# Sixteen images on two lanes: instructions numbered by their place in an image's course, images set 820 units apart, instead of by program order

## The chip, the cores and the metric

The kernel runs on one core of a Trainium2 chip. The metric is the device time of one execution in microseconds (us), lower is better. Engines are named as in the profile: PE (matrix multiplies), DVE (vector), ACT (activations), POOL (GpSimd) and SP (which here only issues DMAs).

## The reference, cut to what matters

The input is sixteen images of 56 x 56 tokens with 128 channels, float32. Each image goes through four residual layers, and nothing is shared between images:

```python
x = x + window_attention(_gn(x))   # 64 windows of 7x7, shifted, 4 heads
x = x + triangle(_gn(x))           # layer norm, gated product over one axis, layer norm, gate
x = x + fourier(_gn(x))            # spectral Q, K, V; 32-head attention; inverse transform; 2 spectral MLP layers
x = x + bilinear(_gn(x))           # SiLU MLP, 3x7 convolutions, per-token 16x16 products
```

`_gn` is a group norm over 32 groups of 4 channels. All arithmetic is float32.

## The kernel before, in words

`tile_blocks` writes out all sixteen images, one after the other, as straight-line code of 5065 numbered instructions each: load, window attention (from number 58), triangle (from 980), Fourier (from 1797), bilinear with the store (from 3668). These numbers are counted within an image, in the order in which the Python code issues them.

Image b uses **lane** `b % 2`. A lane has its own working storage: one arena of 17152 floats per partition (pool `arena`, one buffer), five small row tiles (`w2`), eight statistics tiles, and half of the PSUM banks (`psb`, two buffers, and `psd`, one). So two images can be under way at a time, one on each lane, and image b+2 can begin its arena work only when image b gives up the arena at its end. The lanes share the engines and the DMA queues. Each lane alone is a chain: within an image a stage needs the result of the one before, and inside a stage small buffers hold loops to two or three steps ahead.

Where the pieces of a stage stand, by line of the kernel before:

- window attention: eight window rows (loop over `wi`), L536 (normalise, on DVE and POOL), L538 to L607 (products and transposes on PE). It moves no data but the image.
- triangle: L628 to L722, products L678 and L698, no DMA.
- Fourier: the statistics and column modes (L907), `attention` with the products L1093, the spectral loop of eight steps, where POOL issues two table loads for each of 64 tiles (L1201), DVE multiplies them (L1203) and PE reduces them (L368 and L371, the helper `together`), then inverse transforms and two MLP layers (`operator`, L989, L945).
- bilinear: `project` (L1315 to L1366), `kept` (a tile is copied by ACT and written to DRAM eight times, L1316), `spread` (L1378), `contract` (SP loads the replicated tile, L1411, DVE multiplies, L1414, PE reduces through `together`).

**What sets the order.** The program is built with `schedule_with_timeline_sim=True`. At build time a list scheduler lays out each engine's queue: when an engine falls free in its model of time, of the instructions whose inputs and buffers are ready the one with the lowest number goes next. The number is `tc.cur_priority`, counted up by one with each instruction issued. In the kernel before nothing sets it, so it is program order: every instruction of image b has a lower number than every instruction of image b+1. The queues that come out are fixed; on the chip each engine runs its own in order and waits where a semaphore is not there yet.

Of the kernel before, what the change touches and what calls it, by code (L numbers as in the profile page):

```python
# [54 lines left out]
ROWC = NW * WIN  # L55
NEG = -1.0e30
SN = math.sqrt(28.0 * 64.0)


def _rho(r, cut):  # L60
# [247 lines left out]
def tile_blocks(ctx: ExitStack, tc: tile.TileContext, ins, out, at, stages=(0, 1, 2, 3)):  # L308
# [17 lines left out]
    ps2 = [pool(f"ps2_{k}", 1, space=PSUM) for k in range(2)]  # L326

    lane = [0]
    count = [0]

    def uid(s):
# [117 lines left out]
    def store_image(b, xt):  # L449
        for q in range(NCH):  # L450
# [8 lines left out]
                in_=t[:TT, :].rearrange("p (a c) -> p a c", a=4),  # L459
            )  # L460

    env = dict(locals())
    blocks = [_window_attention, _triangle, _fourier, _bilinear]
    run = {s: blocks[s](env) for s in stages}
    for b in range(NB):
        lane[0] = b % 2
        xt = load_image(b)
        done = False
        for s in stages:
            done = run[s](b, xt)  # L470
        if not done:
            store_image(b, xt)
# [7 lines left out]
def _window_attention(env):  # L480
    e = _Env(env)
# [34 lines left out]
    def run(b, xt):  # L516
# [8 lines left out]
        for k in range(2):  # L525
            nc.gpsimd.memset(ar[:, k * half_arena + ROWC : k * half_arena + 408], 0.0)
        for wi in range(NW):
            o = wi % 2 * half_arena
            xw, qt, vt, st, atn, ot = (
                ar[:, o + a : o + a + n]  # L530
# [84 lines left out]
def _triangle(env):  # L615
    e = _Env(env)
    nc, mm, tt, ts, act, C, W, bc = e.nc, e.mm, e.tt, e.ts, e.act, e.C, e.W, e.bc
    eps = e.persistent("eps1", [P, 1], 1e-5)
    HC = 32

    def layer_norm(chunk, dst, sqs, lw, lb):


        for q in range(NCH):
            d, sq = dst[:, q * CH : (q + 1) * CH], sqs[:, q * CH : (q + 1) * CH]
            src = chunk(q)
            p = e.psb()
            mm(p[:, :CH], lhsT=C("cen"), rhs=src, start=True, stop=True)  # L628
            act(sq, p[:, :CH], AF.Square)  # L629
            nc.vector.tensor_copy(d, p[:, :CH])  # L630

        pv = e.psb()
        e.together(
            dict(
                out=pv[32 * (q % 4) : 32 * (q % 4) + 32, :CH],
                lhsT=C("oh")[:, 1 - q // 4 : 33 - q // 4],
                rhs=sqs[:, q * CH : (q + 1) * CH],
                start=q < 4,
                stop=q > 2,
            )  # L640
            for q in range(NCH)
        )
        rs = e.w2()
        act(rs[:, :CH], pv[:, :CH], AF.Sqrt, bias=eps)
        nc.vector.reciprocal(rs[:, :CH], rs[:, :CH])
        for q in range(NCH):
            d = dst[:, q * CH : (q + 1) * CH]
            p = e.psb()
            row = 32 * (q % 4) + q // 4
            mm(p[:, :CH], lhsT=C("ident")[:, row : row + 1].to_broadcast([P, P]), rhs=rs[:, :CH], start=True, stop=True)  # L650
            tt(d, d, p[:, :CH], ALU.mult)
            act(d, d, AF.Identity, bias=W("ln")[:, lb : lb + 1], scale=W("ln")[:, lw : lw + 1])

    def run(b, xt):
        nm, rs = e.group_norm(xt)
        ar = e.arena()
        xh = ar[:, 0:3144]
        nc.gpsimd.memset(xh[:, NTOK:], 0.0)

        def normed(q):  # L660
            t = e.w2()
            ts(t[:, :CH], xt[:, q * CH : (q + 1) * CH], nm, rs, ALU.add, ALU.mult)
            return t[:, :CH]

        sqs = ar[:, 10312 : 10312 + NTOK]
        layer_norm(normed, xh, sqs, 0, 1)

        l3, r3 = (ar[:, o : o + T * HC].rearrange("p (c i) -> p i c", i=T) for o in (3144, 4936))  # L670
        o3 = ar[:, 6728 : 6728 + 64 * T].rearrange("p (j c) -> p c j", c=64)
        for part in range(2):
            for g in range(T // 8):
                p = e.psd()
                for i in range(8):
                    c0 = (8 * g + i) * T
                    for half, w in ((0, "w1a"), (64, "w1b")):
                        mm(  # L678
                            p[half : half + 64, i // 4, i % 4 * P : (i % 4 + 1) * P],
                            lhsT=xh[:, c0 : c0 + 64],  # L680
                            rhs=W(w).rearrange("p (k c) -> p k c", c=64)[:, :, HC * part : HC * part + HC],
                            start=True,
                            stop=True,
                        )
                pv = p.rearrange("p a (i c) -> p (a i) c", c=P)
                sg = e.w2()
                s3 = sg.rearrange("p (i c) -> p i c", c=64)
                act(s3, pv[:, :, 64:128], AF.Sigmoid)
                tt(l3[:, 8 * g : 8 * g + 8, :], pv[:, :, 0:32], s3[:, :, 0:32], ALU.mult)
                nc.vector.scalar_tensor_tensor(  # L690
                    r3[:, 8 * g : 8 * g + 8, :], pv[:, :, 32:64], 1.0 / T, s3[:, :, 32:64], ALU.mult, ALU.mult
                )
            for g in range(4):
                for half in (0, 64):
                    p = e.psb()
                    s = slice(half, half + T)
                    for c in range(8):
                        mm(p[s, c * T : (c + 1) * T], lhsT=l3[s, :, 8 * g + c], rhs=r3[s, :, 8 * g + c], start=True, stop=True)  # L698
                    dst = o3[s, 8 * (4 * part + g) : 8 * (4 * part + g + 1), :]
                    src = p[s, :CH].rearrange("p (c j) -> p c j", j=T)  # L700
                    if half:
                        nc.scalar.copy(dst, src)
                    else:
                        nc.vector.tensor_copy(dst, src)

        on = ar[:, 3144 : 3144 + NTOK]
        on3 = on.rearrange("p (i j) -> p j i", j=T)
        for g in range(T // 8):
            p = e.psb()
            for j in range(8):  # L710
                for half in (0, 64):
                    s = slice(half, half + T)
                    mm(p[half : half + 64, j * T : (j + 1) * T], lhsT=o3[s, :, 8 * g + j], rhs=C("ident")[s, half : half + T], start=True, stop=True)
            nc.scalar.copy(on3[:, 8 * g : 8 * g + 8, :], p[:, :CH].rearrange("p (j i) -> p j i", i=T))
        layer_norm(lambda q: on[:, q * CH : (q + 1) * CH], on, sqs, 2, 3)
        for q in range(NCH):
            s = slice(q * CH, (q + 1) * CH)
            pg, py = e.psb(), e.psb()
            mm(pg[:, :CH], lhsT=W("gout"), rhs=xh[:, s], start=True, stop=True)
            mm(py[:, :CH], lhsT=W("pout"), rhs=on[:, s], start=True, stop=True)  # L720
            sg = e.w2()
            act(sg[:, :CH], pg[:, :CH], AF.Sigmoid)  # L722
            tt(sg[:, :CH], py[:, :CH], sg[:, :CH], ALU.mult)
            tt(xt[:, s], xt[:, s], sg[:, :CH], ALU.add)

    return run


def _fourier(env):
    e = _Env(env)  # L730
# [145 lines left out]
    def inorm(y, k):  # L876

        _, rs = centered(y)
        ts(rs, rs, sc[:, k : k + 1], None, ALU.mult)
        scaled(y, y, rs, k)  # L880
# [144 lines left out]
    def attention(uv, ar):  # L1025
# [3 lines left out]
        for s in range(2):  # L1029
# [4 lines left out]
            t = e.w2()  # L1034
# [7 lines left out]
        t = e.w2()  # L1042
# [20 lines left out]
        for name in ("dx", "dya", "dyb"):  # L1063
# [6 lines left out]
            else:  # L1070
                t = e.w2()
# [9 lines left out]

        n = 0
        for bank in range(2):
            sp = e.psb()
            for l0 in (0, 4):
                for c in range(2):
# [41 lines left out]
        for g in range(2):  # L1128
            p = e.psb()
            for i in range(4):  # L1130
                q = 4 * g + i
# [7 lines left out]
            ts(by_row(dst)[:, s], by_row(xt)[:, s], nm, rs, ALU.add, ALU.mult)  # L1139

    def run(b, xt):
        nm, rs = e.group_norm(xt)
        ar = e.arena()
        xa = ar[:, 7056:10640]
# [8 lines left out]


        x3 = ar[:TT, : 3 * NM].rearrange("p (k n) -> p k n", k=3)
        for g in range(8):
            p = e.psb()
            for i in range(4):
# [28 lines left out]
        spec = x3[:, 0, :]  # L1187
        n = 0
        for q in range(8):
            s = slice(q * STEP, (q + 1) * STEP)  # L1190
            if q % 2:
                pa, pb = e.psb(), e.psb()
# [4 lines left out]
            for two in range(8):  # L1197
                t = slots[n % 8]
# [28 lines left out]
            nc.scalar.copy(spec[:, s], p)  # L1227


        y = ar[:, NM : NM + NTOK]  # L1230
        normed(xt, nm, rs, y)
        y3 = y.rearrange("p (t j) -> p j t", j=T)
# [12 lines left out]
        def residual(t0, p):  # L1245
            d = y[:, t0 * T : (t0 + 8) * T]
            tt(d, p, d, ALU.add)

        vs = ar[:, 5376 : 5376 + 4 * CH]
        inverse(ar, [spec], residual, vs)  # L1250
        an = ar[:, 5376:8960]
# [4 lines left out]
        p12 = ar[:, 8960:12544]  # L1256
        f = ar[:, 0:3584]
        vs = ar[:, 3584:5376]
        operator(ar, an, "mw0r", "mw0i", f, p12, f, vs, 3)
        nc.gpsimd.memset(by_row(f, True), 0.0)  # L1260
        for q in range(NCH):
            an8, f8 = (by_row(t)[:, 8 * q : 8 * q + 8] for t in (an, f))
            stt(f8, an8, sc[:, 12:13], f8, ALU.mult, ALU.add)
            act(f8, f8, AF.Gelu, bias=shift)
        m = an
        operator(ar, f, "mw1r", "mw1i", m, p12, m, vs, 4, sc[:, 14:15])
        for q in range(NCH):
            m8, f8 = (by_row(t)[:, 8 * q : 8 * q + 8] for t in (m, f))
            stt(m8, f8, sc[:, 14:15], m8, ALU.mult, ALU.add)
        inorm(m, 5)  # L1270
        for q in range(NCH):
            x8, m8 = (by_row(t)[:, 8 * q : 8 * q + 8] for t in (xt, m))
# [5 lines left out]
def _bilinear(env):  # L1278
    e = _Env(env)
# [9 lines left out]
    part = 96 * PLANE // P // 3  # L1289
# [7 lines left out]
        return bass.AP(tensor=t.tensor, offset=t.offset + start, ap=[list(d) for d in dims])  # L1297

    def run(b, xt):
        nm, rs = e.group_norm(xt)  # L1300
        ar = e.arena()
        kv_dram = padded[e.lane[0]]
# [151 lines left out]
        queries, kern, feat = {q: project(q) for q in range(2)}, {}, {}  # L1454
        spread(0, 0)
        for q in range(NCH + 4):
            if 0 <= q - 4:
                last(q - 4, *feat.pop(q - 4))
            if q + 2 < NCH:
# [39 lines left out]
```

## Time and profile before

| | |
|---|---|
| median of 5 runs | 13248.37 us |
| lowest, highest | 13231.01, 13284.84 us |
| profiled execution: time, span | 13248.37 us, 13246.3 us |
| mean granted TensorE clock | 0.859 |
| PE busy, share of the span | 10304.3 us, 78% |
| DVE busy | 9629.6 us, 73% |
| ACT, POOL busy | 3848.2 us (29%), 1619.6 us (12%) |
| DMA moved | 2105.99 MB, mean 159 GB/s |

The span is what the profile covers; the profiled execution took 2.1 us more than its span, and was the median run. Busy times of different engines overlap. A stretch "a:b" is in us from the start of the span. The first records of the even images (lane 0) start at 18, 1577, 3196, 4773, 6442, 8101, 9773 and 11354 us, those of the odd images (lane 1) at 22, 1647, 3285, 4966, 6670, 8359, 9954 and 11618 us; image 14 ends at 13036 us and image 15 at 13243 us. The images 2k and 2k+1 are called pair k+1, so there are pairs 1 to 8, and stretch k+1 runs from the start of image 2k to that of image 2k+2 (the eighth to the end).

### The profile page before, as it was taken

What the parts mean: (1) busy time and instruction counts of PE and PEld (TensorE: products, weight loads), DVE (VectorE), ACT (ScalarE), POOL (GpSimd) and SP (SyncE); (2) the same over time, 40 slices, a digit from 0 to 9 for tenths busy, and PEclk for the clock granted to TensorE, in tenths of its full rate; (3) what the DMA queues carried; (4) which work ended last, traced back from release to release, by engine and by line L of the source; (5) the groups of instructions that cost most, each with busy time, mean ns of one, the idle gap of its engine ahead of it and who ended that gap; (6) DMA issues with size and microseconds to landing.
All of it is one profiled execution on the core that took longest, in us unless ns stands there. A gap on an engine that the chain in (4) does not pass through costs nothing. (4 is left out here: it accounts for less than half of the span.)

```text
span 13246.3 us, 203312 instructions
## 1 busy us (share of the span) xinstructions
PE 10304.3 (78%) x82624; PEld 5717.4 (43%) x82624; DVE 9629.6 (73%) x13985; ACT 3848.2 (29%) x6643; POOL 1619.6 (12%) x3098
## 2 busy tenths in 40 slices
PE   7887688876877777877778777788777887778876
PEld 4443254532544335444354443444335443355432
DVE  7776868768677686676767767777686777767777
ACT  4223141321423214223242232422224222232221
POOL 0130002200022000220002200022000220002200
PEclk9888898888988888887888878998888888888888
DMA  1256904478044780446814458243680447804478
GB/s 35 66 174 228 320 4 118 122 256 295 1 125 120 248 292 11 122 114 222 292 38 124 116 192 292 68 124 116 227 306 19 125 123 240 280 27 121 127 239 290
DMA packets 1091764, 2105.99 MB, mean 159 GB/s; under 512 B 98320, under 2 KB 974096, under 8 KB 1089680
## 3 DMA queue, kind: packets, MB, share of 16 engines
q1 hardware_dynamic: 560000, 823.95, 18.9%
q0 software_dynamic: 165120, 629.61, 17.3%
q10 hardware_dynamic: 365712, 639.44, 13.3%
q8 instruction: 654, 10.72, 0.3%
q14 instruction: 278, 2.28, 0.1%
HBM read 1412.73 MB, written 667.03 MB: 157 GB/s over the span
## 5 line engine op out<-in xcount | busy, mean ns | idle before, releaser
L1414 DVE TENSOR_TENSOR arena<-arena 128x1792 f32<-128x1792 f32 x1344 | 2661.4, 2020 | 685.0 <-DMA arena<-dy 325.9
L1203 DVE TENSOR_TENSOR arena<-arena 112x1344 f32<-112x1344 f32 x1024 | 1570.0, 1553 | 338.2 <-DMA arena<-table 331.0
L371 PE MATMUL psb<-arena,cst 128*32 128x448 f32 x9792 | 1554.8, 662 | 0.8 <-ACT arena L629 0.8
L368 PE MATMUL psb<-arena,cst 128*32 128x448 f32 x1408 | 808.1, 662 | 801.4 <-DVE arena L1414 708.9
L1201 POOL DMA_DIRECT2D arena<-table x2048 | 1065.6, 522 | 2628.8 <-PE psb L1116 674.0
L371 PE MATMUL psb<-arena 112*64 112x224 f32 (+2 forms) x4864 | 1246.9, 525 | 0.0
L368 PE MATMUL psb<-arena 112*64 112x448 f32 (+1 forms) x1280 | 696.6, 630 | 368.4 <-DVE arena L1093 191.6
L371 PE MATMUL psd<-arena 112*64 112x224 f32 (+1 forms) x3072 | 758.1, 470 | 0.0
L368 PE MATMUL psd<-arena 112*64 112x448 f32 x1024 | 561.7, 634 | 177.2 <-DVE arena L1203 156.2
L371 PEld LDWEIGHTS psb<-arena 112*64 112x64 f32 (+1 forms) x4864 | 434.7, 152 | 509.2 <-issue 506.3
L1093 DVE TENSOR_TENSOR arena<-w,coef 128x1792 f32<-128x1792 f32 x256 | 507.5, 2021 | 193.6 <-PE psb L371 176.1
L368 PEld LDWEIGHTS psb<-arena,cst 128*32 128x32 f32 x1408 | 119.0, 119 | 1167.4 <-DVE arena L1414 850.1
L1399 ACT COPY arena<-psd 128x896 f32<-128x896 f32 x336 | 304.1, 906 | 1032.3 <-DVE arena L1414 582.3
L678 PE MATMUL psd<-wgt,arena 128*64 128x128 f32 x7168 | 505.4, 289 | 105.1 <-DVE arena L690 91.7
L371 PEld LDWEIGHTS psb<-arena,cst 128*32 128x32 f32 x9792 | 366.0, 124 | 470.3 <-issue 447.9
L371 PE MATMUL psd<-arena,wgt 128*32 128x448 f32 x2688 | 513.1, 605 | 44.0 <-DMA arena<-padded 43.6
L678 PEld LDWEIGHTS psd<-wgt,arena 128*64 128x64 f32 x7168 | 439.5, 143 | 214.7 <-issue 132.9
L907 PE MATMUL psb<-cst,arena 128*128 128x64 f32 (+1 forms) x2688 | 441.1, 336 | 93.6 <-ACT arena L917 73.5
L368 PE MATMUL psd<-arena,wgt 128*32 128x448 f32 x896 | 439.1, 607 | 64.7 <-DMA arena<-padded 41.1
L907 PEld LDWEIGHTS psb<-cst,arena 128*128 128x128 f32 x2688 | 426.3, 249 | 139.0 <-ACT arena L917 82.5
L1315 ACT COPY w<-psb 128x448 f32<-128x448 f32 x336 | 178.8, 532 | 995.8 <-PE psb L371 655.8
L589 PE MATMUL psb<-cst,arena 128*49 128x128 f32 x2048 | 345.2, 326 | 152.0 <-DVE arena L584 91.2
(302 smaller groups left out, 19590.5 us busy)
## 6 DMA issues: line engine op xcount, KB each, us to landing
arena<-table POOLq DMA_DIRECT2D x2048, 294.0 KB, 8.6
dy<-w ACTq DMA_DIRECT2D x336, 1792.0 KB
arena<-dy SPq DMA_DIRECT2D x1344, 448.0 KB
arena<-padded SPq DMA_DIRECT2D x896, 162.8 KB
w<-x SPq DMA_DIRECT2D x112, 224.0 KB
out<-w SPq DMA_DIRECT2D x112, 224.0 KB
padded<-w ACTq DMA_DIRECT2D x336, 62.0 KB
arena<-arena POOLq DMA_DIRECT2D x16, 784.0 KB, 10.1
```

Of the source, the lines that this page charges most:

```text
L368: done = mm(**first)
L371: mm(**kw)
L589: nc.tensor.transpose(p[:WIN, i * P : (i + 1) * P], s3[:, 4 * g + i, :], C("ident"))
L678: mm(p[half : half + 64, i // 4, i % 4 * P : (i % 4 + 1) * P], lhsT=xh[:, c0 : c0 + 64], rhs=W(w).rearrange("p (k c) -> p k c", c=64)[:, : ...
L907: mm(p[:, 2 * i * nl : 2 * (i + 1) * nl], lhsT=src[:, t * P : (t + 1) * P], rhs=fc, start=True, stop=True)
L1093: tt(t4, bc(ys[c][:, l0 : l0 + 4, :], 1, 8), bc(coef[:, c, h0 : h0 + 8, l0 : l0 + 4], 3, T), ALU.mult,)
L1201: nc.gpsimd.dma_start(out=t[hh * T : (hh + 1) * T, :], in_=bc(tflat[q, two, hh], 0, T))
L1203: tt(t4, bc(x3[:, :, s], 1, 2), t4, ALU.mult)
L1315: nc.scalar.copy(t[:, :CH], p[:, :CH])
L1399: nc.scalar.copy(z, p[:, :, :CH])
L1414: tt(t4, bc(rep, 2, 2), bc(z, 1, 2), ALU.mult)
```

## The change

A helper `at_time(t)` sets the scheduler's number to 100 times the sum of an image's origin and a place t in its course; the origin of image b is 1000 + 820 b. The stages call it with the place at which their next piece stands, from 0 (load) to 1590 (the last of the eleven steps of the bilinear loop). Between two calls the number counts up by one for each instruction, as before. No instruction is added, removed or altered; the buffers and the dependencies stay.

```diff
+BEAT, LEAD, LAG = 100, 1000, 820
...
+    origin = [0]
...
+    def at_time(t):
+
+        tc.cur_priority = int(BEAT * (origin[0] + t))
+
...
     for b in range(NB):
         lane[0] = b % 2
+        origin[0] = LEAD + b * LAG
+        at_time(0)
         xt = load_image(b)
...
         for wi in range(NW):
+            e.at_time(20 + 25 * wi)
...
     def run(b, xt):
+        e.at_time(225)
...
     def run(b, xt):
+        e.at_time(475)
...
         for q in range(8):
+            e.at_time(646 + 19 * q)
...
     def run(b, xt):
+        e.at_time(1120)
...
         for q in range(NCH + 4):
+            e.at_time(1170 + 42 * q)
```

The shown calls are, from above: the load, the window rows, the start of the triangle, the start of Fourier, its spectral loop, the start of the bilinear stage and its loop. The other calls stand in the same way at the parts of a stage: 300 and 340, 380 and 440 in the triangle; 540 and 575, 620, 800, 858, 910, 1000 and 1085 in Fourier.

By these numbers image b+2 (origin 1640 above that of b) at place t goes ahead of image b+1 at place t' as long as t' - t is over 820; before, image b+1 always went ahead of image b+2. Between image b, at place t, and image b+1, at t', image b goes ahead as long as it is less than 820 further on; before, always.

More of the change, by code (lines that the diff above doesn't have):

```diff
@@ L672, in run @@
         for part in range(2):
+            e.at_time(300 + 40 * part)
             for g in range(T // 8):
@@ L707, in run @@
         on3 = on.rearrange("p (i j) -> p j i", j=T)
+        e.at_time(380)
         for g in range(T // 8):
@@ L715, in run @@
         layer_norm(lambda q: on[:, q * CH : (q + 1) * CH], on, sqs, 2, 3)
+        e.at_time(440)
         for q in range(NCH):
@@ L1083, in attention @@
         for bank in range(2):
+            e.at_time(540 + 35 * bank)
             sp = e.psb()
@@ L1155, in run @@
         x3 = ar[:TT, : 3 * NM].rearrange("p (k n) -> p k n", k=3)
+        e.at_time(620)
         for g in range(8):
@@ L1227, in run @@
             nc.scalar.copy(spec[:, s], p)
+        e.at_time(800)
         y = ar[:, NM : NM + NTOK]
@@ L1247, in residual @@
             tt(d, p, d, ALU.add)
+        e.at_time(858)
         vs = ar[:, 5376 : 5376 + 4 * CH]
@@ L1258, in run @@
         vs = ar[:, 3584:5376]
+        e.at_time(910)
         operator(ar, an, "mw0r", "mw0i", f, p12, f, vs, 3)
@@ L1265, in run @@
         m = an
+        e.at_time(1000)
         operator(ar, f, "mw1r", "mw1i", m, p12, m, vs, 4, sc[:, 14:15])
@@ L1269, in run @@
             stt(m8, f8, sc[:, 14:15], m8, ALU.mult, ALU.add)
+        e.at_time(1085)
         inorm(m, 5)
```

## The prediction

> **What bounds the kernel now.** I read the head of the page first, then the busy times in stretches of one pair each, then short stretches for the stages, then the waits of PE and DVE.
>
> The head of the page:
>
> ```profile
> span 13246.3 us, 203312 instructions
> PE 10304.3 (78%) x82624; PEld 5717.4 (43%) x82624; DVE 9629.6 (73%) x13985; ACT 3848.2 (29%) x6643; POOL 1619.6 (12%) x3098
> ```
>
> No engine is full. The best two engines lie idle for 22% and 27% of the span, so what counts is how well the work of the two lanes fills each other's gaps. Two short stretches, from the windows view, show what there is to fit together (columns: stretch, us, then busy us and count of PE, PEld, DVE, ACT, POOL; then granted clock, DMA share, GB/s):
>
> ```profile
> 1900.00:2000.00 100.00, 92.18 (x1240) 67.28 (x1240) 51.39 (x79) 50.36 (x69) 0.00 (x0) 1.00 0.01 2
> 1400.00:1500.00 100.00, 65.76 (x464) 24.42 (x464) 80.78 (x59) 14.89 (x24) 0.98 (x2) 0.88 1.02 364
> ```
>
> In the first both lanes are in the triangle: PE 92%, DMA 1%. In the second both are in the bilinear stage: PE 66%, DMA full. The lanes run nearly in step, both asking for the same thing. The waits view says what that costs DVE at its two big loops, and PE behind one of them:
>
> ```profile
> DVE arena L1203 <- DMA arena<-table: 331.0, 403, 5.0
> DVE arena L1414 <- DMA arena<-dy: 325.9, 176, 7.2
> PE psb L368 <- DVE arena L1414: 708.9, 329, 9.3
> ```
>
> So lanes half a course apart would have something to gain. The eight stretches of one pair each (cut where an even image starts), same columns:
>
> ```profile
> 18.00:1577.00 1559.00, 1205.45 (x10068) 681.24 (x10072) 1176.12 (x1755) 460.61 (x811) 196.17 (x387) 0.90 0.49 160
> 1577.00:3196.00 1619.00, 1265.09 (x10268) 707.42 (x10264) 1190.58 (x1736) 475.99 (x825) 194.17 (x386) 0.87 0.49 159
> 3196.00:4773.00 1577.00, 1220.14 (x9928) 676.60 (x9920) 1136.96 (x1691) 464.14 (x807) 200.41 (x384) 0.87 0.48 148
> 4773.00:6442.00 1669.00, 1297.99 (x10212) 725.88 (x10216) 1183.88 (x1723) 482.94 (x830) 202.63 (x386) 0.84 0.49 153
> 6442.00:8101.00 1659.00, 1298.81 (x10195) 722.58 (x10188) 1178.64 (x1719) 478.68 (x822) 201.93 (x384) 0.84 0.48 152
> 8101.00:9773.00 1672.00, 1322.76 (x10651) 719.85 (x10650) 1242.58 (x1788) 498.36 (x854) 208.11 (x389) 0.87 0.52 169
> 9773.00:11354.00 1581.00, 1245.74 (x10010) 701.01 (x10008) 1151.95 (x1696) 467.37 (x810) 206.56 (x383) 0.85 0.49 153
> 11354.00:13246.00 1892.00, 1448.35 (x11309) 782.80 (x11307) 1364.99 (x1868) 518.82 (x884) 209.09 (x390) 0.84 0.54 174
> ```
>
> A stretch holds a little more or less than one pair's work, so I divide its length by its DVE time (third busy column): 1.326, 1.360, 1.387, 1.410, 1.408, 1.346, 1.372, 1.386. The code of every pair is the same; only the interleaving of the lanes differs. The same work costs between 1.35 and 1.41 in stretches 4 to 8, and 0.064 on a pair's DVE time (9625.7 / 8 = 1203 us) is 77 us. This spread, not the half course, is what the change moves.
>
> **The change, part by part.**
>
> *What it does to the order.* Nothing is added, so the question is how the built queues differ. Among images b and b+1 the elder is never 820 ahead: the odd images start 4 to 264 us after the even ones (fronts of the records). So the elder still wins every tie. The right flips only while image b+1 finishes and b+2 has begun: there t' is over 1400 and t below 250, and the younger now goes first. These overlaps last 79, 101, 202, 237, 266, 190 and 272 us (end of image 1 at 1656 against start of image 2 at 1577, and so on): 1347 of 13246 us. Even there the number decides only where both have something ready.
>
> I laid the two builds' DVE queues side by side. How far the odd image has come, as the number of its last DVE instruction out of 5065, when the next even image begins on DVE: before 4870, 4780, 4389, 4335, 4181, 4487, 4181; after 4870, 4780, 4389, 4389, 4335, 4181, 4335. Half a course would be about 2500. The lanes do not go apart: the change does not do what its description says. It shuffles the pairs.
>
> *Which pairs it shuffles.* The share of a stretch's DVE instructions that must be moved to turn one order into another (those outside the longest common order): stretch 1 unchanged, 2: 5%, 3: under 1%, 4: 12% from its own; stretch 5 of the new kernel is like none (25% from the old 4th, 30% from the old 5th); its 6th is the old 5th (1% moved); its 7th is the old 8th (9%); its 8th is nearest to the old 5th (30%) and the old 8th (34%). PE's queue says the same (3%, 0%, 12%, 22%, 1%, 9%, 28%). For scale, two different late pairs of the kernel before are 33 to 45% apart. The good old stretches 6 (1.346) and 7 (1.372) have no counterpart in the new kernel, except where one arises anew in its 5th or 8th.
>
> *The sum,* on 1203 us of DVE time per stretch:
> - Stretches 1 to 4: their own ratios, 0. The 12% in the fourth could be worth 0.12 x 77 = 9 us, either way.
> - Stretch 5: unknown. Bounds: the best and the worst of the late rows, 1.346 and 1.410, against 1.408 before: -75 to +3 us. I take the mean of rows 4 to 7, 1.384, since it lies near none of them: (1.384 - 1.408) x 1203 = -29 us.
> - Stretch 6: the old fifth's 1.408 in place of 1.346: +75 us.
> - Stretch 7: the old eighth's 1.386 in place of 1.372: +16 us, 9 us either way. That row holds image 15's last 210 us, alone on the chip; without them it is (1892 - 210) / (1364.99 - 143.81) = 1.377, which gives +6. I take +6, as the new seventh has no such tail (143.81 is DVE's busy time of 13036 to 13246).
> - Stretch 8: its bilinear half is in the same order as before, its first half is new. Bounds 1.346 and 1.410 against 1.386: -49 to +28 us; I take 0, as its two nearest rows, 1.408 and 1.386, lie on and above its own.
>
> Sum: -29 + 75 + 6 = +52 us. The profiled execution is the median run (13248.37 us, 2.1 us outside the span), so 13248.4 + 52 = **13300 us**.
>
> *What is at nothing.* The number is a build-time thing and issues nothing. 158 table loads on ACT instead of 163, at 1.283 us each, is 6.4 us on an engine busy 29%: covered by its idle time; if it were not, a gain of 6 us. Waits that stand as instructions of their own go from 2315 to 2341 on PE at 51 ns (the row at the image load): 1.3 us at most. The DMA issues are the same, in another order: on SP's queue an issue stands 2.2 places from where it stood on average (36 at most), on POOL's 0.8. An `arena<-dy` load that is moved behind another lane's `arena<-padded` load on SP holds up L1414; that price is within the pair ratios, which contain such waits.
>
> *The clock.* In the rows above the granted clock is 0.84 where the ratio is 1.41, 0.87 at 1.387, 1.360 and 1.346, and 0.90 at 1.326: loosely ordered.
>
> [...] If no ratio were inherited, stretches 5 to 8 would all take the mean 1.384, and the sum would be (4 x 1.384 - 1.408 - 1.346 - 1.372 - 1.386) x 1203 = +29 us, 13277 us. That no run here shows yet; the five runs before lie within 0.4% of each other, which speaks for orders that repeat their times.
>
> **The rivals.**
> - *It cancels out.* The late pairs are draws from one bag, new ones as good as old: 13248 us, within 40. For it: half of stretches 5 and 8 is new. Against: stretch 6 is to 99% a known bad one.
> - *The new stretches are good ones (faster).* If the 5th and the 8th both come out at 1.346, as the old 6th did, they give -75 and -49: 52 + 29 - 75 - 49 = -43 us, 13205 us. It decides from the point where the two together stand 92 us below my values (52 - 92 = -40); 46 + 49 = 95 is the most they have. For it: such a pair arose once in five late ones. Against: both have to.
> - *The lanes do part (faster by far).* If the chip ran them half a course apart, the DVE waits for DMA at the two loops (331.0 + 325.9 us) could go: 13248 - 657 = 12591 us. Against it: the queues are fixed at build, and in them the odd image is at 82% or more of its instructions when the next even one starts.
>
> **How the numbers follow.** No change can be told from one below about 0.3%, 40 us, here. My case (13300, with 50 to 60 us of doubt from stretches 5 and 8): 0.62; cancelling: 0.24; the good stretches: 0.12; parted lanes: 0.02. In my own case some 0.09 falls below 13288, which leaves 0.53; of the cancelling case 0.03 ends above that and 0.02 under 13208. Slower by over 0.3%: 0.53 + 0.03 = 0.56. Same: 0.09 + 0.19 = 0.28. Faster: 0.12 + 0.02 + 0.02 = 0.16. Range: everything at its low end is 52 - 46 - 49 - 9 - 9 = -61, at its high end 52 + 32 + 28 + 9 + 9 = +130; all ends at once are unlikely, and the far low end takes in the good stretches: 13195 to 13370.
>
> **What would show it.** The profile after, cut at its even images: ratios near 1.326, 1.360, 1.387 in the first three; 1.41 in the fourth and sixth, 1.38 in the seventh. The odd image should still be in its bilinear stage when the next even one starts, and DVE's waits for the table and the replicated tiles should stay near 331 and 326 us. I am wrong if the sixth stretch comes out near 1.35, as then an order does not carry its time with it; or if the two lanes show different stages throughout.

## The result, and the profile after

No difference: median 13265.31 us over 45 runs (13214.74 to 13319.19), against 13262.7 us over 87 runs of before (13198.57 to 13364.52). The ratio is 1.0000, 95% interval 0.9991 to 1.0009, so within 12 us either way. The forecast was 13300 us, 52 us more than the first five runs of before, with slower as the likeliest outcome (0.56). The change measured is +3 us. The time lies in the forecast's range and within the 40 us of its rival "it cancels out".

The runs of before spread further than the first five had shown: standard deviation 33 us, 0.25%. Their median of 13248.37 us was a draw from that, 14 us under that of all 87.

The head of the page after, and the same two short stretches (both lanes in the triangle; both in the bilinear stage):

```profile
span 13228.7 us, 203274 instructions
PE 10246.2 (77%) x82624; PEld 5687.9 (43%) x82624; DVE 9627.5 (73%) x13985; ACT 3840.7 (29%) x6638; POOL 1609.6 (12%) x3098
```

```profile
1900.00:2000.00 100.00, 94.58 (x1195) 67.62 (x1194) 49.28 (x80) 47.00 (x65) 0.00 (x0) 0.97 0.01 2
1400.00:1500.00 100.00, 69.36 (x488) 25.53 (x480) 79.92 (x59) 16.87 (x26) 0.51 (x1) 0.86 1.00 358
```

The lanes do the same things at the same times as before. The waits (lines 1203, 1414 and 368 are now 1220, 1437 and 370):

```profile
DVE arena L1220 <- DMA arena<-table: 330.2, 407, 3.5
DVE arena L1437 <- DMA arena<-dy: 321.6, 159, 9.2
PE psb L370 <- DVE arena L1437: 736.7, 342, 15.3
```

331 and 326 us before, 330 and 322 us after: nothing was parted. (That they agree so closely is partly luck. In the further profiles below the wait for the table is 312 and 379 us before and 335 to 363 us after, that for the replicated tiles 327 to 346 and 309 to 333 us.) The eight stretches, cut at the first record of each even image (columns as in the prediction; the third busy column is DVE's):

```profile
18.00:1574.00 1556.00, 1213.98 (x10077) 679.87 (x10078) 1177.71 (x1756) 460.88 (x812) 196.67 (x387) 0.88 0.49 161
1574.00:3191.00 1617.00, 1272.87 (x10257) 708.56 (x10255) 1192.02 (x1735) 475.48 (x825) 199.20 (x386) 0.86 0.49 159
3191.00:4758.00 1567.00, 1217.56 (x9946) 679.33 (x9946) 1137.88 (x1691) 463.77 (x807) 196.35 (x384) 0.87 0.48 150
4758.00:6421.00 1663.00, 1279.82 (x10332) 709.73 (x10332) 1201.60 (x1742) 480.18 (x832) 207.26 (x386) 0.87 0.51 159
6421.00:8036.00 1615.00, 1262.93 (x10208) 704.10 (x10205) 1178.19 (x1730) 478.75 (x826) 199.82 (x386) 0.86 0.50 156
8036.00:9672.00 1636.00, 1280.49 (x10179) 717.32 (x10180) 1175.39 (x1709) 477.46 (x821) 199.24 (x384) 0.84 0.48 154
9672.00:11343.00 1671.00, 1305.54 (x10479) 736.14 (x10477) 1215.59 (x1765) 494.35 (x846) 207.18 (x388) 0.86 0.51 163
11343.00:13228.70 1885.70, 1413.04 (x11164) 752.90 (x11160) 1345.31 (x1846) 508.53 (x870) 203.35 (x388) 0.85 0.54 169
```

Length over DVE time: 1.321, 1.357, 1.377, 1.384, 1.371, 1.392, 1.375, 1.402. The sixth, whose order is the old fifth's, is the highest of the fourth to seventh, as forecast, but at 1.392 and not 1.408; and the fourth, mostly the old order, is 1.384 and not 1.410. So an order may not give the same ratio twice. That was the first thing to measure.

### The profile page after: what moved, and what is told of

Read it like the earlier page. It is cut to its first block, busy times and chain, and to the rows that moved or that the text cites. A ratio compares the mean times of both kernels' runs of the same rounds, so it can differ in the third digit from the quotient of the medians.

```text
span 13228.7 us, 203274 instructions
## 1 busy us (share of the span) xinstructions
PE 10246.2 (77%) x82624; PEld 5687.9 (43%) x82624; DVE 9627.5 (73%) x13985; ACT 3840.7 (29%) x6638; POOL 1609.6 (12%) x3098
## 5 line engine op out<-in xcount | busy, mean ns | idle before, releaser
L689 PE MATMUL psd<-wgt,arena 128*64 128x128 f32 x7168 | 500.9, 288 | 112.8 <-DVE arena L701 93.4
L689 PEld LDWEIGHTS psd<-wgt,arena 128*64 128x64 f32 x7168 | 437.2, 142 | 218.2 <-issue 134.1
```

The costliest lines, as they stand in the source:

```text
L689: mm(p[half : half + 64, i // 4, i % 4 * P : (i % 4 + 1) * P], lhsT=xh[:, c0 : c0 + 64], rhs=W(w).rearrange("p (k c) -> p k c", c=64)[:, : ...
```

## The experiments

### How far does an order carry its time? Both kernels again

The kernel before was profiled two more times and the changed one three more, unchanged.

> The kernel before, unchanged, profiled a second time and cut into the same eight stretches (an even image's start to the next even image's start), each stretch's length divided by DVE's busy time in it. Theory A, that the order of a stretch carries its time, as the prediction had it: the ratios come back within 0.010 of 1.326, 1.360, 1.387, 1.410, 1.408, 1.346, 1.372, 1.386, and the sixth is again the lowest of the last five. Theory B, that the spread among the late stretches is an execution's chance: the last five differ from their first values by up to 0.03, in no order, while the first three (the lanes closer together) stay below or at the mean of the late ones.

> A third profile of the kernel before. The first two gave for stretches 4 to 8: 1.410, 1.408, 1.345, 1.373, 1.386 and 1.399, 1.385, 1.361, 1.354, 1.396. If order carries a part of the time, stretches 4 and 5 are again above 1.385 and 6 and 7 below 1.375. If all of it is chance, one of these four is on the other side.

> The changed kernel, unchanged, profiled a second time; its first profile gave the ratios 1.321, 1.357, 1.377, 1.384, 1.371, 1.392, 1.375, 1.402. Theory A: they come back within 0.010, and the sixth (whose order is the old fifth's) stays the highest of stretches 4 to 7. Theory B: stretches 4 to 8 move by up to 0.03 and the sixth is not the highest.

> A third profile of the changed kernel, for its stretch ratios (so far 1.321, 1.357, 1.377, 1.384, 1.371, 1.392, 1.375, 1.402 and 1.325, 1.362, 1.357, 1.400, 1.360, 1.376, 1.381, 1.390). The three profiles of before have stretches 4 and 5 at 1.399 to 1.410 and 1.385 to 1.408, 6 and 7 at 1.345 to 1.367 and 1.354 to 1.373. If a copied order carries its time, the sixth here (the old fifth's order) is 1.385 to 1.408. If it carries part of it, 1.37 to 1.385. If none, 1.35 to 1.37.

> A fourth profile of the changed kernel, same expectations as the third. The fifth, new in its order, has been 1.371 and 1.360, under the 1.384 that the prediction took: again below 1.38 if the new order is a good one, 1.38 to 1.41 if that was chance.

Measured, length over DVE time of each stretch:

| stretch | before: 3 profiles | mean | after: 4 profiles | mean | difference x 1203 us |
|---|---|---|---|---|---|
| 1 | 1.326 1.311 1.321 | 1.319 | 1.321 1.325 1.323 1.324 | 1.323 | +5 |
| 2 | 1.360 1.397 1.387 | 1.381 | 1.357 1.362 1.369 1.373 | 1.365 | -19 |
| 3 | 1.387 1.374 1.375 | 1.379 | 1.377 1.357 1.368 1.381 | 1.371 | -10 |
| 4 | 1.410 1.399 1.402 | 1.404 | 1.384 1.400 1.391 1.389 | 1.391 | -16 |
| 5 | 1.408 1.385 1.398 | 1.397 | 1.371 1.360 1.371 1.373 | 1.369 | -34 |
| 6 | 1.346 1.361 1.367 | 1.358 | 1.392 1.376 1.390 1.380 | 1.385 | +32 |
| 7 | 1.372 1.354 1.361 | 1.362 | 1.375 1.381 1.381 1.383 | 1.380 | +21 |
| 8 | 1.386 1.396 1.400 | 1.394 | 1.402 1.390 1.405 1.416 | 1.403 | +11 |

The differences add up to -10 us, which agrees with the ratio of 1.0000 within 12 us. One order's ratio varies between executions by a standard deviation of 0.002 to 0.019 (2 to 23 us a stretch). For scale, the old fifth and sixth stretches in the third profile of before:

```profile
6452.00:8098.00 1646.00, 1294.67 (x10187) 721.54 (x10188) 1177.14 (x1720) 476.93 (x822) 202.09 (x384) 0.84 0.48 153
8098.00:9800.00 1702.00, 1337.09 (x10655) 725.77 (x10654) 1245.08 (x1786) 497.54 (x854) 207.24 (x389) 0.86 0.52 167
```

1646 / 1177.14 = 1.398 and 1702 / 1245.08 = 1.367, where the first profile had 1.408 and 1.346. What one profile showed as a gap of 0.062 is 0.031 here and 0.024 in the second profile. Theory A asked for every ratio to come back within 0.010 and for the old sixth to be the lowest of the late ones again. It was too strong: the second stretch of before moved by 0.037, and in its second profile the seventh was lower than the sixth. In the second profile of the changed kernel, too, the sixth is not the highest of stretches 4 to 7, as theory B had it. But theory B's "in no order" was wrong: in the third profile of before stretches 4 and 5 are again above 1.385 and 6 and 7 below 1.375, as expected if the order carries a part. In the changed kernel the new fifth stays below 1.38 in all four profiles. Its sixth was 1.390 in the third profile ("carried") and 1.380 in the fourth ("carried in part").

The means say more. The old fifth's order has a mean of 1.397 in its old place and 1.385 in its new one, as the sixth. The old sixth, which it replaces, has 1.358. Each of these means is uncertain by 0.004 to 0.007 (one standard error). So the copied order clearly did not turn into another 1.358, and the 0.012 that it lost is not clear of noise. The old eighth without image 15's lone end has 1.377, 1.382 and 1.388 in the three profiles, a mean of 1.382; its order, as the new seventh, has a mean of 1.380. An order thus carries its mean as far as these profiles can tell, while a single execution of it strays.

### What if the lanes really part? A gate for lane 1

The change was described as setting the images half a course apart, and the built queues did not do it. One true dependency does:

```diff
+    gate = cpool.tile([P, 1], F32, tag="gate", name="gate")
...
-            act(xt[:, q * CH : (q + 1) * CH], p[:, :CH], AF.Identity, bias=W("bout0"))
+            act(xt[:, q * CH : (q + 1) * CH], p[:, :CH], AF.Identity, bias=gate if b == 1 else W("bout0"))
...
         normed(xt, nm, rs, y)
+        if b == 0:
+            stt(e.gate, y[:, :1], 0.0, W("bout0"), ALU.mult, ALU.add)
```

> The changed kernel with one true dependency more: image 1's load takes its bias from a copy that image 0 writes after its spectral loop, so that lane 1 starts half a course after lane 0. In the built queues the odd image is then at number 2351 to 2600 of 5065 when the next even one starts, throughout: the lanes are parted as the change says it wants. Theory 'parting pays': DVE's waits for the table and the replicated tiles (331 and 326 us) fall by more than half, and the stretches in the middle (second to seventh) have ratios of 1.29 to 1.33 instead of 1.37; with half a course run alone at either end the time is 13000 to 13300 us. Rival 'it makes no odds': ratios of 1.36 to 1.40 in the middle, and the lone halves come on top, 13450 to 13800 us. Rival 'the mix is worse': ratios over 1.40 and more than 13800 us.

> The kernel before (program-order numbers) with the same dependency as the parted kernel: image 1's load waits for a copy that image 0 writes after its spectral loop. Its queues keep the lanes parted too: the odd image is at number 1930 to 2066 of 5065 when the next even one starts, against 2351 to 2600 with the change's numbers. So the two parted kernels compare the numbers where the lanes are far apart and the change's rule really decides. If the numbers matter there, the two differ by over 1% (the change's numbers took 13874 us); if they do not, this one takes 13805 to 13943 us and its middle ratios are again 1.40 to 1.42.

The parted kernel with the change's numbers took 13874.11 us, ratio 1.0445 (1.0415 to 1.0476); odd images start 724 to 801 us after the even ones. With program-order numbers it took 14014.21 us, 1.0552 (1.0527 to 1.0577). One of the middle stretches of the first from the windows view, and its DMA waits of DVE (L1440 is the bilinear multiply, L1221 the spectral one; columns of a wait: us in total, times, longest):

```profile
3157.00:4845.00 1688.00, 1289.75 (x10316) 708.63 (x10314) 1190.24 (x1739) 500.93 (x846) 201.08 (x384) 0.85 0.51 155
```

```profile
DVE arena L1440 <- DMA arena<-dy: 480.4, 134, 16.6
DVE arena L1221 <- DMA arena<-table: 349.5, 373, 3.2
```

The ratio here is 1688 / 1190.24 = 1.418; stretches 2 to 7 have a mean of 1.411 against 1.380 before. The wait for the replicated tiles rises from 326 to 480 us, and that for the table, at 350 us, stays within the 312 to 379 us of before. "Parting pays" has fallen, and "the mix is worse" fits both by its ratios (over 1.40) and by its time (over 13800 us). Of the 611 us over 13263, the middle has (1.411 - 1.380) x 1203 x 6 = 224 us; the remaining 387 us lie at the two ends, where one lane runs alone:

```profile
13283.00:13870.00 587.00, 373.14 (x2350) 181.44 (x2346) 312.94 (x422) 122.53 (x209) 30.43 (x56) 0.73 0.49 164
```

587 us for 313 us of DVE work is a ratio of 1.88, at a granted clock of 0.73.

The replicated tiles are not where most of the middle's loss stands. Over stretches 2 to 7 alone, all of DVE's waits for ACT rise from 745 us before to 1054 us, those for DMA only from 537 to 595 us, and those for PE fall from 1291 to 1185 us. The wait that grows most over whole executions is that of the triangle's product with a sigmoid (L689 before, L701 in the parted kernel):

```profile
DVE arena L689 <- ACT w L688: 197.1, 126, 7.5
DVE arena L701 <- ACT w L700: 419.4, 136, 9.5
```

With program-order numbers the middle is the same within what profiles vary by (1.417), though its waits rise in another mix (ACT +93, DMA +99, PE +93 us): no one wait is shown to be the cause of the middle's loss. The lone end is longer: image 14 ends at 13150 us and image 15 at 14007 us. There the change's numbers do work as written: with them the spacing is more even (in the third pair the odd image starts 732 us after the even one instead of 1031), and they save 1.0% of the parted kernel, 127 of the 140 us in the first and last stretch. Of the expectations each got a half: the times differ by just the 1% set for "the numbers matter", and the middle ratios stay at 1.40 to 1.42, as set for "they do not".

A shorter distance, with the gate written at the start of image 0's Fourier stage and 475 units between images:

```diff
-BEAT, LEAD, LAG = 100, 1000, 820
+BEAT, LEAD, LAG = 100, 1000, 475
...
         normed(xt, nm, rs, xa)
+        if b == 0:
+            stt(e.gate, xa[:, :1], 0.0, W("bout0"), ALU.mult, ALU.add)
```

> As the parted kernel with the change's numbers, but lane 1 is released at the start of image 0's Fourier stage and the images are set 475 units apart, a little over a quarter of a course. If the cost of distance grows from the natural lag (ratio 1.37) to the half course (1.41 in the middle), the middle ratios are 1.38 to 1.40 and with a shorter lone part at either end (about 210 us by the parted kernel's 360) the time is 13500 to 13650 us. If there is a best distance between the two, middle ratios of 1.31 to 1.35 and 13100 to 13350 us. If any distance other than the natural one is bad, 1.42 or more and over 13750 us.

13503.2 us, ratio 1.0166 (1.0141 to 1.0190), odd images 551 to 562 us behind. Stretches 2 to 7: 1.391, 1.384, 1.374, 1.373, 1.376, 1.372, mean 1.378, the same as before's 1.380. The time fits "the cost grows with the distance" (13500 to 13650 us), but the middle ratios lie at the lower edge of its 1.38 to 1.40: the middle neither gains nor loses, and the 240 us are the lone ends. This holds although the wait for the replicated tiles is longer here than in the parted kernel, so that wait alone does not set the ratio:

```profile
DVE arena L1440 <- DMA arena<-dy: 597.7, 162, 22.2
```

### The other direction: images closer together

The distance is one constant, so it was turned down: to 0 as shown, and in the same way to 50, 100 and 200.

```diff
-BEAT, LEAD, LAG = 100, 1000, 820
+BEAT, LEAD, LAG = 100, 1000, 0
```

> The changed kernel with the images set 0 instead of 820 units apart: whichever lane is behind goes first, and in the built queues the odd image has run all but the last few of its 5065 instructions when the next even one starts, so the lanes are locked in step. Theory 'lag costs': the first stretch, where the lanes are 4 us apart, has a ratio of 1.326 and the ratio rises with the lag over the first three; locked lanes then hold 1.32 to 1.34 in all eight stretches, 12780 to 12950 us. Rival 'the interleaving does not matter': 13262 us, within 40, ratios near 1.37. Rival 'in step they collide': both lanes are in the loops that wait for DMA at once, DVE's waits for the table and for the replicated tiles rise well over 331 and 326 us, and the time is 13350 to 13700 us.

> The changed kernel with the images set 100 units apart: the lane behind goes first once it is more than 100 behind. In the queues the odd image is at 4809 to 4911 of 5065 when the next even one starts, so the lag is small throughout but never zero. If what cost 4.8% at distance 0 is the closeness of the lanes, this lies between: 13350 to 13700 us, ratios 1.38 to 1.43, DVE's wait for the table between 331 and 664 us. If it was only the exact lock, with both lanes asking for the same at the same moment, 13262 us within 60 and a table wait near 331 us. If a small lag is best, as the first stretches (1.32 to 1.38) had it, under 13200 us.

> Images set 50 units apart. In the queues the odd image is at 4840 to 4930 of 5065 when the next even one starts, nearly as with 100 (4809 to 4911), which was 0.7% faster than before. If the small lag makes the gain, partly by the short end in which lane 1 is alone, it is the same here: 13110 to 13230 us. If the lock at 0 already reaches here, over 13350 us.

> Images set 200 units apart; in the queues the odd image is at 4584 to 4663 of 5065 in the late pairs, between 100 (4809 to 4911) and 820 (4181 to 4389). If the time follows the lag it is between them, 13180 to 13260 us, and the last 100 to 150 us have lane 1 alone instead of 67 (at 100) or 230 (at 820). If only a lag under some 100 units pays, 13262 within 30. If the order of the pairs is a draw each time, anywhere from 13150 to 13350 us with no relation to the lag.

| distance set | odd image starts after the even one, stretches 4 to 8 | time, us | ratio to before, 95% | table loads on ACT |
|---|---|---|---|---|
| 0 | -11 to -14 us | 13911.12 | 1.0483 (1.0447 to 1.0520) | 68 |
| 50 | 43 to 61 us | 13093.96 | 0.9874 (0.9835 to 0.9912) | 103 |
| 100 | 73 to 74 us | 13173.46 | 0.9928 (0.9902 to 0.9953) | 125 |
| 200 | 120 to 129 us | 13226.31 | 0.9972 (0.9950 to 0.9994) | 135 |
| 820 (the change) | 184 to 259 us | 13265.31 | 1.0000 (0.9991 to 1.0009) | 158 |
| program order (before) | 180 to 264 us | 13262.7 | 1 | 163 |

Each ratio is to runs of before made beside it, 11 to 17 of them for the distances 0 to 200, so it is not exactly the quotient of the times shown.

From 820 down to 50 the time falls with the distance; at 0 it jumps by 6%. The version at 50 beats both kernels by 1.3%. No value between 0 and 50 was run. At 100 and 200 the times came where a gain from a small lag was expected (under 13200 us; 13180 to 13260 us); at 50 the gain is larger than the 13110 to 13230 us expected. That the order of the pairs is a mere draw at each distance is unlikely with four distances in a row but not excluded: at 50, with odd images 43 to 61 us behind, the ratios of stretches 4 to 8 still range from 1.343 to 1.403 in its one profile. The span and the waits at 50, in an execution that was the longest of its six:

```profile
span 13139.8 us, 203264 instructions
```

```profile
DVE arena L1220 <- DMA arena<-table: 394.1, 424, 3.4
DVE arena L1437 <- DMA arena<-dy: 162.0, 118, 6.9
```

The two DMA waits are 394 + 162 = 556 us, 101 less than the 657 of before. And at 0:

```profile
DVE arena L1220 <- DMA arena<-table: 663.6, 460, 3.1
DVE arena L1437 <- DMA arena<-dy: 210.1, 126, 16.3
```

Here the wait for the table doubles, to 664 us: locked, the two lanes are in the spectral loop 11 to 14 us apart. "In step they collide" is half right: the wait for the replicated tiles, which it expected to rise, fell from 326 to 210 us, and the loss went past its 13700 us; "lag costs", which expected under 12950 us, has fallen at this point. The rise of the two waits together, 874 - 657 = 217 us, is only a third of the some 640 us lost. And the waits alone don't order the rows: at 200 they are 348 + 202 = 550 us, as few as at 50, with a gain of only 0.3%. DVE's waits summed by what ended them (all rows of the waits view, profiled executions) show what these two waits leave out:

| | for PE, us | for ACT, us | for DMA, us | together |
|---|---|---|---|---|
| before | 1703 | 1006 | 745 | 3454 |
| distance 50 | 1451 | 1235 | 653 | 3339 |
| distance 0 | 2049 | 1123 | 973 | 4145 |

At 50 the waits for PE fall by 252 us, more than those for DMA, and those for ACT rise by 229 us; at 0 half of the rise is for PE. The lone end shrinks too, from 210 us to

```profile
13097.00:13140.00 43.00, 18.45 (x112) 4.90 (x112) 26.27 (x17) 1.60 (x3) 0.00 (x0) 0.68 0.48 157
```

but 210 us of lane 1 alone did 143.81 us of DVE work, which would have taken an estimated 143.81 x 1.38 = 198 us beside another lane: shortening that end is worth 12 us at most. What makes a distance of 50 better than 200 was not taken apart further.

## Why the prediction was right or wrong

- *The change does not do what it says.* Right. The even image leads the odd one by 4 to 259 us in the profile after, the two DMA waits are unchanged to within 5 us, and stretches 1 to 3 are within 0.010 of their old ratios in the first profile.
- *The right flips only in the overlaps, so it shuffles the pairs.* Right as far as it was tested: with the gate, which keeps the lanes far apart, the two sets of numbers differ by 1%; without it by nothing. The shuffle itself shows in the means: stretches 4 and 5 became quicker, 6 and 7 slower.
- *Stretch 6, +75 us.* This is the term that was mis-sized, and the forecast's rise hung on it. It has the right sign and measured +32 us. The term was the difference of the highest row but one and the lowest row of the late five in a single execution. Repeated, the row of 1.408 has a mean of 1.397 and the row of 1.346 one of 1.358: rows picked for being extreme came back toward the mean, and the term would have been (1.397 - 1.358) x 1203 = +47 us. The other 15 us, from 1.397 to the 1.385 of the order in its new place, are not clear of their noise of 9 us. So the mechanism, that a copied order brings its time, is not refuted; what was wrong was to read an order's time off one execution.
- *Stretch 5, -29 us:* measured -34. *Stretch 7, +6:* +21; here too the copied order kept its time (1.382 without the lone end, 1.380 as the new seventh), and it was the row replaced, 1.372 in one execution, that has a mean of 1.362. *Stretch 8, 0:* +11. *Stretch 4, 0 with 9 either way:* -16.
- *Stretches 1 to 3 at nothing:* -24 us together, on orders that are 0 to 5% different. With three and four profiles, the difference of a stretch's two means is uncertain by 5 to 14 us, so most of these small terms can't be told from 0. From +52 to the -10 us that the table adds up to, 43 of the 62 us are stretch 6, and the rest is spread over terms of this size.
- *Where luck came in.* The forecast stood on a base of 13248.37 us, 14 us under the median of 87 runs; without that it would have been 13315 us, 49 over the result. And the sum came to nothing because quicker stretches (4 and 5, -50 us) happened to stand against slower ones (6 and 7, +53 us). That is the number of the rival "it cancels out", but not its draws from one bag: the late orders keep different means.
- *"The five runs before lie within 0.4%, which speaks for orders that repeat their times."* It did not follow: eight stretches that each vary by 2 to 23 us still sum to a total that varies by only 33 us (before) or 25 us (after). The 13277 us that the prediction gave for the case that no ratio is inherited is nearer to the 13265 measured than the 13300 chosen, but the stretches don't bear that case out. The old fifth's order had 0.84, 0.85 and 0.84 in three profiles and 0.84, 0.86, 0.84 and 0.85 in its new place, so its low granted clock did come along (the old sixth, which it replaced, had 0.87, 0.86 and 0.86). Where the spread of an order's ratio between executions comes from, no run here shows.
- *The rival of parted lanes, 12591 us.* Its condition did not come about, and the price had the wrong sign: made to part, the kernel took 13874 us, and the two DVE waits for DMA rose from 657 to 830 us, those for ACT by more. Reading "both lanes ask for the same thing" off the two short stretches as something to be gained by half a course was wrong.

## What to carry to other kernels

Before a difference of a few per cent between stretches of one profile is carried over as a property of their code, profile the same kernel again: here a gap of 0.062 shrank to 0.024 and 0.031. A scheduler's number decides only among what is ready; whether lanes part is seen in the built order, and here parting them by half a course took a dependency. And when a constant sets a distance, try both directions: the half course cost 4.5% (over half of it at the lone ends), a distance of 50 gained 1.3%, and 0 cost 4.8%.

## What the runs showed that was not expected

- How often ACT loads a function table, at 1.283 us each, depends on how the lanes are interleaved. Locked lanes need 68 loads, the kernel before 163, lanes half a course apart 282 with the change's numbers and 244 with program order. In the parted kernel the bilinear SiLU alone has 103, against 20 in the profile of before:

```profile
L1354 ACT ACT_TABLE_LOAD x103 | 132.1, 1283 | 19.0 <-issue 13.5 <-DMA padded<-w 2.8 <-ACT arena L662 1.2
```

```profile
L1328 ACT ACT_TABLE_LOAD x20 | 25.7, 1283 | 3.8 <-ACT w L1315 1.9 <-ACT arena L917 1.0 <-DMA arena<-dy 0.6
```

  The (282 - 163) x 1.283 = 153 us of it are at most a part of what parting cost, on an engine that was 29% busy before; how much of it stood in the way was not measured. It need not cost anything: at the distance of 475 there are 241 loads, and the middle ratio is that of before. Going from 163 loads to 103 at a distance of 50 is 77 us of ACT time in the same sense.
- In the last 587 us of the parted kernel a lane alone runs at a ratio of 1.88 where two have 1.38, with the granted clock at 0.73 instead of 0.86. So each us in which the second lane is not there is dear at the ends, but not everywhere alike: the last 210 us of before, in the bilinear loop, have 210 / 143.81 = 1.46.
